# Two first loads of the second graph pass, converted to fp32r by GpSimd's transfers on their way from DRAM

## The chip, the cores and the metric

The kernel runs on one core of one Trainium2 chip. A core has TensorE (matmul), VectorE, ScalarE, GpSimd and SyncE, which work side by side and wait for each other on semaphores, and 16 DMA engines that serve the transfers issued by SyncE, ScalarE and GpSimd. The metric is the device time of one execution in microseconds (us), the median of the runs shown. In the profile PE is TensorE, PEld its weight loads, DVE is VectorE, ACT is ScalarE, POOL is GpSimd, SP is SyncE; SPq, ACTq and POOLq are the DMA issues of an engine.

## The reference

Two layers of a graph network over 6250 nodes of 128 features and 206,250 edges, each behind a layer norm and a relu, each added to its input.

```python
h = jnp.maximum(_layernorm(x, axis=-1), 0.0)
x = x + _L0_gnn_ref(h, src, dst, W, b)       # deg**-0.5 scaling, sum over edges, relu, @ W.T + b
h = jnp.maximum(_layernorm(x, axis=-1), 0.0)
x = x + _L1_gnn_ref(h, [src, dst], edge_type, ...)
# _L1_gnn_ref:
msg = h[src] @ W_msg.T + b_msg + edge_embed[clip(edge_type, 0, 8)]
messages = segment_sum(msg, dst, 6250)
return gru_cell(messages, h, W_ih, W_hh, b_ih, b_hh)
```

## The kernel before, in words

The sums over edges are done as matrix products. The nodes are padded to 6272, which is 49 blocks of 128. The kernel builds the 6272 x 6272 matrix of edge counts (`adj`) once, in bf16, from one-hot rows on TensorE, and uses it twice.

**First pass.** It goes through the destination columns in 25 tiles: one of 128 and 24 of 256 columns. For each tile the counts are built, copied to SBUF by ScalarE (L855), widened to fp32r in seven pieces of seven source blocks (`wide1`, L947, by VectorE and ScalarE in turn; the seventh piece, `wide_last`, by a GpSimd transfer, L943), and multiplied (L811) with the first table `tab1`, whose seven tiles each hold seven source blocks in two terms (an fp32 value split in two fp32r numbers): 14 matmuls for each piece. The counts are also stored to DRAM as `adj_d` (L954, by SyncE), cut into 13 tiles of destination columns for the second pass: one of 384, eleven of 512 and one of 256. L868, L872 and L876 end the first layer for a tile, L881 adds its result to `xs`, and L883 to L900 compute the norm's mean and scale.

**Second pass.** For each of the 13 tiles (`BACK`), `blocks(c, nd)` gives a function `block(q)` that brings piece q, seven source blocks by the tile's columns: a load from `adj_d` by SyncE into `piece` (L1007, one of four buffers), then a conversion to fp32r into `wide` (one of three buffers) by VectorE (L1018) or, after the first tile and for even q, by ScalarE (L1011). Row sums of the counts (`leave`, L999) are taken beside it for a final consistency test. `sums` multiplies the pieces with the second table `tab2` (L811): 7 pieces x 14 matmuls for a tile. A GRU cell follows for each tile: h from the table (L1051), its transpose (L1055, copied by L1057 to `hT`), products with `whh_sb` (L1061), with the type counts (L1071) and with the sums (L1066, L1073), two sigmoids (L1078, L1079), a tanh (L1085), elementwise steps (L1081 to L1090), a transpose back (L1094), the addition (L1096) and the store (L1101). `second_layer` is a generator whose stages are laid among the next tile's matmuls.

**Between the passes.** The second table is made from `xs` in seven steps: seven ScalarE activations (L1030) for each, then a VectorE cast (L1031) and a VectorE subtraction (L1032). After steps 1, 3 and 5 the kernel calls `first(0)`, `first(1)` and `first(2)`, the first tile's pieces 0, 1 and 2; the other four are called from `sums`. `whh_sb` is loaded from ScalarE's queue at L1036.

**What sets the order.** In the second pass and between the passes, the order of the instructions of each engine is made by a scheduler when the program is built; in the first pass it is mostly as written. Waits follow from the tiles' memory: a tile placed over an earlier one waits until that one's last reader is done. The `wide` pool lies on the right side of SBUF, where `tab1` was. GpSimd issues only the indirect loads of the prologue and the 25 `wide_last` transfers before the seam, and none after it.

Of the kernel before, what the change touches and what calls it, by code (L numbers as in the profile page):

```python
# [12 lines left out]
F32R = mybir.dt.float32r  # L13
# [8 lines left out]
P = 128  # L22
# [24 lines left out]
HP = 7  # L47
# [225 lines left out]
def by_matrix(  # L273
# [22 lines left out]
    nc = tc.nc  # L296
# [8 lines left out]
    adj_d = [dram.tile([P, NB, n], BF16, name=f"adj_d{c}") for c, (_, n) in enumerate(BACK)]  # L305
# [85 lines left out]
    with tc.tile_pool(name="pro", bufs=1) as pro, tc.manual_schedule(engines={mybir.EngineType.DVE}):  # L391
# [13 lines left out]
        for c in range(NCH):  # L405
            lo, hi = c * CB, min((c + 1) * CB, full)
            nc.sync.dma_start(
                out=xs[:, lo:hi, :], in_=x[lo * P : hi * P, :].rearrange("(b p) f -> p b f", p=P)
# [30 lines left out]
        for h in range(2):  # L439
            nc.gpsimd.indirect_dma_start(  # L440
                out=span[:, h, :],
                out_offset=None,
                in_=dst.rearrange("p t -> (p t)").unsqueeze(1),
# [68 lines left out]
        for k0 in range(0, NT // P + 1, 4):  # L512
# [26 lines left out]
            if n == P:  # L539
                nc.sync.dma_start(  # L540
                    out=flat[k0 * P : k1 * P, :].rearrange("(k p) e -> p k e", p=P),
                    in_=turned[:, k0:k1].rearrange("p k h f e -> p k (h f e)"),
# [281 lines left out]
    with tc.tile_pool(name="adj_even", bufs=1, reuse_waits="tile") as adj_even, tc.tile_pool(  # L824
        name="wide1", bufs=3, reuse_waits="tile"
    ) as wide1p, tc.tile_pool(
        name="ev_ps", bufs=1, space=PSUM, reuse_waits="tile"
# [158 lines left out]
    with early_p as tab2a, tc.tile_pool(name="gru_a", bufs=2, reuse_waits="tile") as gru_a, tc.tile_pool(  # L986
        name="tab2b", bufs=1, reuse_waits="tile"
    ) as tab2b, tc.tile_pool(name="f2_p", bufs=2, reuse_waits="tile") as f2p, tc.tile_pool(
        name="back", bufs=4, reuse_waits="tile"
    ) as backp, tc.tile_pool(name="gru", bufs=2, reuse_waits="tile") as gru, tc.tile_pool(name="wide", bufs=3, side="right", reuse_waits="tile") as wide, tc.tile_pool(  # L990
        name="gate_ps", bufs=1, space=PSUM
# [6 lines left out]
        def row_sums(q, c, piece):  # L998
            nc.vector.tensor_reduce(leave[:, q * HP : (q + 1) * HP, c], piece, AX.X, ALU.add)  # L999

        def blocks(c, nd):
            pieces = {}

            def block(q):
                if q not in pieces:
                    piece = backp.tile([P, HP, 512], BF16, name="piece")
                    nc.sync.dma_start(out=piece[:, :, :nd], in_=adj_d[c][:, q * HP : (q + 1) * HP, :])  # L1007
                    pieces[q] = wide.tile([P, HP, 512], F32R, name="wide")
                    if c > 0 and q in BY_ACT:
                        for i in range(HP):  # L1010
                            nc.scalar.activation(  # L1011
                                pieces[q][:, i, :nd],
                                piece[:, i, :nd],
                                AF.Copy,
                                accum_out=leave[:, q * HP + i, c : c + 1],
                            )
                    else:
                        nc.vector.tensor_copy(pieces[q][:, :, :nd], piece[:, :, :nd])  # L1018
                        if c > 0:
                            row_sums(q, c, piece[:, :, :nd])  # L1020
                return pieces[q]

            return block

        first = blocks(0, BACK[0][1])
        for c in range(NCH):
            f = f2p.tile([P, CB, H], F32, name="f2")
            for k in range(CB):
                b = c * CB + k
                nc.scalar.activation(f[:, k, :], xs[:, b, :], AF.Relu, bias=sh[:, b : b + 1], scale=rstd[:, b : b + 1])  # L1030
            nc.vector.tensor_copy(tab2[c][:, 0], f)  # L1031
            nc.vector.tensor_tensor(tab2[c][:, 1], f, tab2[c][:, 0].bitcast(F32), ALU.subtract)  # L1032

            if c in (1, 3, 5):
                first(c // 2)
        nc.scalar.dma_start(out=whh_sb, in_=whhT)  # L1036

        def second_layer(d0, nd, acc):
# [104 lines left out]
def gnn_kernel(tc, *args):  # L1143
    with tc.tile_pool(name="bad", bufs=1) as pool:
        bad_i = pool.tile([P, 1], I32, name="bad_i")
        by_matrix(tc, bad_i, *args)
        general(tc, bad_i, *args)
# [47 lines left out]
```

## Time and profile before

| what | value |
|---|---|
| median of 3 runs | 931.22 us (930.29 to 931.83) |
| profiled execution, its own time | 934.99 us |
| its span | 933.2 us |
| granted TensorE clock over the span | 0.96 |
| TensorE busy | 852.5 us (91%) |
| VectorE busy | 799.1 us (86%) |
| ScalarE busy | 712.3 us (76%) |
| GpSimd busy | 54.6 us (6%) |
| DMA q1 (SyncE) / q0 (GpSimd), share of 16 engines | 60.5% / 7.9% |

The busy shares are averages over stages with different limits: a prologue of about 110 us, the first pass to about 551 us, the second pass from there. What an edit between the passes is worth has to be read from the stretch around 550 us and from whether TensorE has idle time after it. In the slices of the page each digit is the busy share of one fortieth of the span in tenths; PEclk is the clock that TensorE was granted.

### The profile page before, as it was taken

The page shows a single profiled execution, that of the slowest core. Times are in us where ns is not written, and L with a number is a line of the kernel's source. Part 1 is how long each engine was busy: PE and PEld are TensorE (multiplying, and loading weights), DVE is VectorE, ACT ScalarE, POOL GpSimd, SP SyncE. Part 2 cuts the span into 40 slices and gives each one's busy share as a digit, 9 for nine tenths or more (in the row PEclk, how much of TensorE's full clock was granted, in tenths as well). Part 3 has the DMA queues.
Part 4 walks back from the last instruction along what each step waited for, and adds up shares of the span by engine and source line. Part 5 has one row for each costly group of instructions (what it writes and reads, how often), then busy time and mean ns, then how long its engine had stood idle before and what let it go on. Part 6 is the DMA issues. An engine that isn't in the chain of part 4 may idle for free.

```text
span 933.2 us, 24704 instructions
## 1 busy us (share of the span) xinstructions
PE 852.5 (91%) x10859; PEld 717.7 (77%) x10859; DVE 799.1 (86%) x835; ACT 712.3 (76%) x1205; POOL 54.6 (6%) x103
## 2 busy tenths in 40 slices
PE   3566499999998999999999979999999999999995
PEld 3354399998997999899999979776777777777775
DVE  5869999999999999999999768998888888877754
ACT  2277898999898899899999984776667676675752
POOL 4561000000000000000000000000000000000000
PEclk9579699999999999999999989999999999999998
DMA  9430177787787689678688798776777667766640
GB/s 283 126 105 32 40 185 238 221 264 232 221 263 233 186 250 276 191 235 273 203 244 274 216 313 289 257 267 211 279 281 243 234 239 264 266 216 225 212 128 23
DMA packets 205664, 203.72 MB, mean 218 GB/s; under 512 B 11178, under 2 KB 190881, under 8 KB 205393
## 3 DMA queue, kind: packets, MB, share of 16 engines
q1 hardware_dynamic: 198904, 173.34, 60.5%
q0 software_dynamic: 6032, 27.43, 7.9%
q8 instruction: 86, 1.41, 0.6%
q10 hardware_dynamic: 612, 1.30, 0.4%
q14 instruction: 30, 0.25, 0.1%
HBM read 95.68 MB, written 83.87 MB: 192 GB/s over the span
## 4 chain that ended last, share of the span: by engine, by line
PE 64%; ACT 14%; DVE 10%; issue 6%; DMA 4%; POOL 1%; another core or an unknown queue 0%; DVEq 0%; SPq 0%; ACTq 0%; POOLq 0%
PE acc L811 45%; ACT adj L855 8%; PE ev L843 7%; DMA piece<-adj_d 3%; ACT wide L947 3%; PE gate L1073 3%; PE gate L1061 3%; DVE wide L1018 2%; PE acc L876 2%; DVE leave L999 1%; PE turn L681 1%; DVE fields L672 1%; ACT f L1030 1%; PE sums L710 1%; DVE hot_l L353 1%
## 5 line engine op out<-in xcount | busy, mean ns | idle before, releaser
L811 PE MATMUL acc<-wide,tab 128*128 128x256 f32 (+2 forms) x3374 | 580.9, 327 | 4.3 <-issue 2.2
L811 PEld LDWEIGHTS acc<-wide,tab 128*128 128x128 f32 x3374 | 489.5, 189 | 65.6 <-issue 13.6
L855 ACT CAST adj<-ev 128x1960 bf16<-128x1960 f32 (+2 forms) x221 | 282.5, 1340 | 35.9 <-PE ev L843 19.9
L1011 ACT ACTIVATE wide<-piece 128x512 fp32r<-128x512 bf16 (+1 forms) x336 | 200.9, 601 | 63.5 <-issue 33.9
L353 DVE TENSOR_TENSOR hot_l<-lo_t,iota 128x3840 bf16<-128x3840 bf16 (+2 forms) x109 | 223.4, 2050 | 5.8 <-PE ev L843 5.7
L999 DVE TENSOR_REDUCE leave<-piece 128x7 f32<-128x3584 bf16 (+2 forms) x43 | 154.9, 3602 | 23.5 <-DMA piece<-adj_d 23.4
L947 ACT CAST wide<-adj 128x1792 fp32r<-128x1792 bf16 (+1 forms) x75 | 126.2, 1682 | 0.0
L843 PE MATMUL ev<-hot_c,hot_l 64*128 64x49 bf16 x6204 | 100.7, 182 | 7.1 <-DVE hot_c L353 3.6
L843 PEld LDWEIGHTS <-hot_l 64*128 64x128 bf16 x6204 | 88.5, 93 | 21.8 <-issue 4.4
L353 DVE TENSOR_TENSOR hot_c<-code_t,iota 128x1500 bf16<-128x1500 bf16 (+2 forms) x109 | 97.4, 893 | 0.0
L1018 DVE CAST wide<-piece 128x3584 fp32r<-128x3584 bf16 (+2 forms) x43 | 82.5, 1920 | 12.3 <-PE acc L811 12.3
L947 DVE CAST wide<-adj 128x1792 fp32r<-128x1792 bf16 (+1 forms) x75 | 80.5, 1087 | 14.4 <-ACT adj L855 13.6
L1011 ACT ACTIVATION_READ_ACCUMULATOR wide<-piece 128x1 f32 x336 | 63.2, 188 | 0.0
L1066 ACT COPY sum_sb<-acc 128x512 f32<-128x512 f32 (+2 forms) x13 | 7.3, 563 | 58.4 <-PE acc L811 58.4
L811 PE MATMUL acc<-wide_last,tab 128*128 128x256 f32 x350 | 48.2, 283 | 0.0
L811 PEld LDWEIGHTS acc<-wide_last,tab 128*128 128x128 f32 x350 | 43.6, 188 | 0.4
L943 POOL DMA_DIRECT2D wide_last<-adj x25 | 13.7, 550 | 447.4 <-PE acc L811 207.9
L1073 PE MATMUL gate<-sum_sb,wsum_sb 128*128 128x512 f32 (+2 forms) x78 | 35.0, 585 | 0.1
L1061 PE MATMUL gate<-hT,whh_sb 128*128 128x512 f32 (+2 forms) x78 | 33.7, 567 | 0.0
L681 PE MATMUL turn<-ident_b,fields 128*128 128x128 bf16 x225 | 20.6, 275 | 13.7 <-DVE fields L672 10.3
L681 PEld LDWEIGHTS <-fields 128*128 128x128 bf16 x225 | 19.0, 128 | 15.8 <-DVE fields L672 12.1
L650 POOL DMA_INDIRECT got<-flat,row_i x25 | 27.4, 1098 | 14.7 <-DVE m_dve L706 7.7
(167 smaller groups left out, 504.4 us busy)
## 6 DMA issues: line engine op xcount, KB each, us to landing
adj_d<-adj SPq DMA_DIRECT2D x24, 3136.0 KB
piece<-adj_d SPq DMA_DIRECT2D x77, 896.0 KB
wide_last<-adj POOLq DMA_DIRECT2D x24, 896.0 KB
piece<-adj_d SPq DMA_DIRECT2D x14, 672.0 KB
piece<-adj_d SPq DMA_DIRECT2D x7, 448.0 KB
out_dram<-res SPq DMA_DIRECT2D x11, 256.0 KB
xs<-in_x_dram SPq DMA_DIRECT2D x6, 448.0 KB
adj_d<-adj SPq DMA_DIRECT2D x1, 1568.0 KB
```

Of the source, the lines that this page charges most:

```text
L353: nc.vector.tensor_tensor(to.rearrange("p j (k t) -> p j k t", t=2), twice.unsqueeze(2).to_broadcast([P, n, m // 2, 2]), of[:, :m].rearran ...
L650: nc.gpsimd.indirect_dma_start(out=got[:, b].rearrange("p r f j -> p (r f j)"), out_offset=None, in_=edges_flat, in_offset=bass.IndirectOf ...
L681: nc.tensor.matmul(turns_[i][:, b, :], fields[:, b * ROWS + r, i].rearrange("p d j -> p (d j)"), ident_b, start=(r == 0), stop=(r == ROWS ...
L811: nc.tensor.matmul(acc[:, : 2 * P].rearrange("f (t n) -> f t n", t=2) if twice else acc[:, :nd], tab[:, s, i, :], a[:, i, :P].unsqueeze(1) ...
L843: nc.tensor.matmul(ps[:, d % banks, slot * NB : (slot + 1) * NB], hot_l[half, t + d // 2, :], hot_c[half, t + d // 2, :NB], start=True, st ...
L855: nc.scalar.copy(adjs[c][:, :, at : at + n].rearrange("p n (j d) -> p n j d", d=banks), ps[:, :banks, : n // banks * NB].rearrange("p d (j ...
L947: make(wides[c][q][:, :, :n], a)
L999: nc.vector.tensor_reduce(leave[:, q * HP : (q + 1) * HP, c], piece, AX.X, ALU.add)
L1011: nc.scalar.activation(pieces[q][:, i, :nd], piece[:, i, :nd], AF.Copy, accum_out=leave[:, q * HP + i, c : c + 1],)
L1018: nc.vector.tensor_copy(pieces[q][:, :, :nd], piece[:, :, :nd])
L1061: nc.tensor.matmul(ps[:, :nd], whh_sb[:, g * H : (g + 1) * H], hT[:, :nd], start=True, stop=(g == 2))
L1073: nc.tensor.matmul(ps[:, :nd], wsum_sb[:, g * H : (g + 1) * H], sum_sb[:, :nd], start=False, stop=True)
```

## The change

For the first tile's pieces 0 and 1, `block` no longer loads bf16 with SyncE and converts with VectorE. It asks GpSimd for a transfer from `adj_d` in DRAM straight into `wide`, which converts bf16 to fp32r on the way. Both calls are placed ahead of the loop that makes the second table. The calls to `first` inside the loop are gone, so piece 2, which had one, is now brought where `sums` asks for it, as pieces 3 to 6 are. Pieces 2 to 6 of the first tile and all later tiles keep the load and the conversion.

```diff
             def block(q):
-                if q not in pieces:
+                if c == 0 and q < 2 and q not in pieces:
+
+                    pieces[q] = wide.tile([P, HP, 512], F32R, name="wide")
+                    nc.gpsimd.dma_start(out=pieces[q][:, :, :nd], in_=adj_d[c][:, q * HP : (q + 1) * HP, :])
+                elif q not in pieces:
                     piece = backp.tile([P, HP, 512], BF16, name="piece")
                     nc.sync.dma_start(out=piece[:, :, :nd], in_=adj_d[c][:, q * HP : (q + 1) * HP, :])
                     pieces[q] = wide.tile([P, HP, 512], F32R, name="wide")
...
         first = blocks(0, BACK[0][1])
+        for q in range(2):
+            first(q)
         for c in range(NCH):
...
             nc.vector.tensor_copy(tab2[c][:, 0], f)
             nc.vector.tensor_tensor(tab2[c][:, 1], f, tab2[c][:, 0].bitcast(F32), ALU.subtract)
-
-            if c in (1, 3, 5):
-                first(c // 2)
         nc.scalar.dma_start(out=whh_sb, in_=whhT)
```

In the built program the scheduler also moves other instructions of the second pass. In the first tile TensorE's order becomes: 14 matmuls of piece 0, one type product (L1071), two of the three products with `whh_sb` (L1061), the matmuls of pieces 1 to 5, the third L1061 product, piece 6; before, the three L1061 products stood together ahead of piece 6 and the type product ahead of piece 3. VectorE's copy of `hT` (L1057) stands after the cast of piece 2; before, it stood after the casts of pieces 0 to 4. On SyncE the loads of pieces 2 and 3, then the three of the type counts, then those of pieces 4 to 6 keep their order behind the two that are gone; since the four `piece` buffers now begin with piece 2, those of pieces 4 and 5 need not wait for a buffer. In tiles 8 to 11 the transposes of the gate output (L1094) stand 18 matmuls behind the L1073 products; before, 28.

## The prediction

> **What bounds the kernel now.** I read the slices and the costliest groups of the page first, then TensorE's waits and its busy time in stretches of the second pass, then the timeline of 547 to 580 us engine by engine, and last the DMA queues us by us. The page and the stretches say who sets the pace:
>
> ```profile
> PE   3566499999998999999999979999999999999995
> PEclk9579699999999999999999989999999999999998
> L811 PE MATMUL acc<-wide,tab 128*128 128x256 f32 (+2 forms) x3374 | 580.9, 327 | 4.3 <-issue 2.2
> 700.00:730.00 30.00, 30.00 (x125) 21.98 (x124) 25.51 (x16) 20.48 (x63) 0.00 (x0) 1.00 0.74 250
> PE tr L1094 <- DVE og L1090: 4.5, 5, 2.8
> ```
>
> The second pass is a queue on TensorE: 30.00 of 30.00 us busy, VectorE 25.5, ScalarE 20.5, DMA 0.74. From 578 us to the end TensorE waits five times, 4.5 us in all, always for the gate output. So a shift of the second pass's start is carried to the end, and work taken from VectorE later buys nothing. The seam between the passes is the one hole:
>
> ```profile
> 547.74 1.82 PE L811 MATMUL acc<-wide_last,tab 128*128 128x256 f32 x14
> 550.58 0.71 PE L876 MATMUL acc<-w_sb,rl 128*128 128x128 f32 x4
> 554.51 0.88 PE L1055 MATMUL tr<-ident,h 128*128 128x128 f32 x3 [3.22 <-DVE sh L893]
> 556.25 10.38 PE L811 MATMUL acc<-wide,tab 128*128 128x384 f32 x42 [0.87 <-DVE rstd L894]
> 566.82 7.69 PE L811 MATMUL acc<-wide,tab 128*128 128x384 f32 x42
> ...
> 553.81 0.55 DVE L1051 TENSOR_TENSOR h<-tab 128x384 f32<-128x384 f32 x1
> 554.28 0.16 DVE L893 TENSOR_TENSOR sh<-sh 128x4 f32<-128x4 f32 x1
> 554.35 1.75 DVE L1018 CAST wide<-piece 128x2688 fp32r<-128x2688 bf16 x1
> 556.02 0.15 DVE L894 SCALAR_TENSOR_TENSOR rstd<-sh,rstd 128x4 f32<-128x4 f32 x1
> ```
>
> Columns: start, duration, engine, line, operation, count. TensorE waits until 554.5 for h, then until 556.25 for the first cast of a piece. Equal groups of 42 matmuls then take 10.38 and 7.69 us. The clock column (last but two) says why:
>
> ```profile
> 552.00:552.25 0.25, 0.00 (x0) 0.00 (x0) 0.25 (x1) 0.25 (x2) 0.00 (x0) 0.69 1.10 326
> 561.75:562.00 0.25, 0.25 (x2) 0.25 (x2) 0.25 (x2) 0.25 (x2) 0.00 (x0) 0.50 1.09 338
> 562.25:562.50 0.25, 0.25 (x3) 0.25 (x2) 0.25 (x1) 0.22 (x1) 0.00 (x0) 0.83 0.41 126
> ```
>
> The granted clock falls to 0.50 at 552.1 and is back at 562.3.
>
> **The change, part by part.**
>
> *Removed.* Two loads of SyncE and two VectorE casts of 1.75 us (3.5 us), the first of which TensorE waits for. Its start now needs the transposes (554.51 + 0.88 = 555.39) and the landed transfer. VectorE's order up to h is the same in both builds, so the 554.5 stays. The second cast is worth nothing by itself: the matmuls of piece 1 follow those of piece 0 without a gap in the trace. Direct gain: 556.25 - 555.39 = 0.86 us.
>
> *Clock.* A 384-column matmul takes 7.69/42 = 0.183 us at full clock. In the group of 10.38 us, 4.3 us lie after 562.3 (23.6 matmuls), so 18.4 take 6.05 us: 0.33 us each. [...] I take 0.4, with ends 0 and 1.5.
>
> *Added: two GpSimd transfers.* In the built program the three wide buffers lie over blocks 1-2, 5-6 and 3-4 of the first table, taken in that order. So transfer 0 waits for the last matmul on block 2 (541.60 plus nine of 6.30/51 us: 542.7; SyncE's second load, which waits for block 3, goes out at 544.65, one block of 1.73 us later: 542.9). Transfer 1 waits for the last matmul of the first pass, 549.5. "Begun ahead of the second table" therefore holds for neither in time. Both wait behind nothing else on GpSimd: its last wide_last, issued 537.60, is before them. Issue:
>
> ```profile
> 112.77 1.00 POOL L943 DMA_DIRECT2D wide_last<-adj  x1 [35.78 <-ACT adj L855]
> 537.60 0.53 POOL L943 DMA_DIRECT2D wide_last<-adj  x1 [16.00 <-PE acc L811]
> q0 software_dynamic: 50, 0.36, 90.4%
> q0 software_dynamic: 16, 0.01, 4.5%
> ```
>
> The first row is the near one, since that transfer also has 896 rows: 1.0 us. The queue lines (packets, MB, share) are of 544 to 545 and 546 to 547: issued at 537.60, this queue moves its bulk from 544 and is done at 546.2, because SyncE's last store (25 KB packets) is ahead in the engines. The transfer of 112.77 starts near 117. So a start lag of 4.2 us; transfer 0 begins at 547.2.
>
> Duration: 896 rows of 768 B in, 1536 B out, 56 per engine. Plain loads run at 326 GB/s, giving 2.1 us as the lower bound. wide_last alternates with the loads packet by packet at about 390 GB/s written; a pair of 1536 + 768 B at 390/16 per engine is 94 ns, so 5.3 us for 56 with a load beside it. I take 5.3, upper end 6.6 (pairs of 118 ns, the two packets one after the other). Transfer 0: 547.2 + 5.3 + 1 for the receipt (wide_last: data to 546.2, used at 547.7 without a wait; 1 us is my estimate) = 553.5, needed at 555.4: hidden, 1.9 us to spare. Transfer 1: 549.6 + 4.2 + 5.3 + 1 = 560.1.
>
> [...]
>
> *Moved by the scheduler.* TensorE now does block 0 (14 matmuls), one type product and two of the three L1061 products, then block 1. Those need hT and whh_sb. VectorE: h ends 554.36, sh, tab L1031 (0.6), the piece-2 cast (1.75; its load is first behind the store on SyncE's queue and shares with transfer 0, landing about 552.6), small ones, tab L1032, tab L1031, hT: 559.2. TensorE arrives at 555.4 + 11 x 0.33 + 3 x 0.183 + 0.3 = 559.9, or 560.6 cold. whh_sb leaves ScalarE's queue 1 us earlier than at 556.21, as the L897 it stands behind does; in before its packets ended in 559 to 560, so about 559. Both hidden by 0.7 to 1.4 us; without that cover, up to 1 us. Then 4 x 0.35 for the two products: block 1 starts at 561.2, transfer 1 is there with 1 us to spare.
>
> On SyncE, the loads of pieces 2 and 3 move up to the places of 0 and 1 (535.89, 544.65); the type loads wait for L876 as before (551.37); pieces 4 and 5 find free buffers and follow at 552.4, where they went out at 556.13 and 558.54. They share the engines with transfer 1, land by 560 and are cast at 564 and 566.3, when wide buffers come free. Cover: 4 us.
>
> Blocks 1 to 6 and the third L1061 product, unhindered, take 6 x 14 x 0.183 + 0.7 = 16.1 us: end of tile 0 at 577.3 with the early clock, 578.2 cold, against 578.9 now (L1066 copies the sum at 578.95).
>
> *Later tiles.* The scheduler's order differs to the end. In tiles 8 to 11 the gate output's transposes (L1094) now stand 18 matmuls behind the L1073 products instead of 28. By ScalarE's three casts, two sigmoids, two casts and the tanh, then three VectorE steps of 0.68, og is ready 14.0 us into the tile; TensorE arrives at 13.65: up to 0.35 us x 4 = 1.4 us of stall. Against it, tile 2 loses 0.9 + 0.3 us at its L1094 now and tile 8 0.41; the new order leaves tile 2's transposes 38 matmuls of room. Net 0, ends -1.6 and +1.4.
>
> **Sum.** -0.86 - 0.4 + 0 = -1.3 us. The profiled execution is 934.99 (span 933.2, 1.8 around it), 3.8 above the median of 931.22; it becomes 933.7, the median 929.9.
>
> **Rivals.**
> *A, slower: transfer 1 becomes the wait.* It starts only at 549.6. If it lags as wide_last did (6.4 us, to 544.0) and runs at the upper 6.6 us, it lands at 563.6. [...] 2.4 + 1.5 - 0.86 = +3.0: 934.3. It decides from a landing at 561.2; beyond 562.1 the gain is eaten. For it: 1.38 MB written where 0.69 was, with the queue 0.90 to 1.1 busy until 554. Against: the 25 KB packets are gone by 546.
> *B, nothing left:* the start moves 0.86 us but the L1094 stalls of tiles 8 to 11 (1.4) come true: 931.4. Speaks for it: every trailing order with few matmuls of room stalled at least once (0.90, 0.22, 0.41).
> [...]
> *D, transfers hidden and also useless*, if h were late anyway: excluded for the first 0.86 us, since the transposes ended at 555.39 and only the cast held the product.
>
> **Chances and range.** Main case 0.37 (929.9), A 0.23, B 0.2, C 0.2. 0.2% is 1.9 us, about what a measurement of this kernel tells from no change. Faster by more: C and a third of the main case; slower: A; the rest between. Main's own range 928.8 to 931.0; with the others 927.3 to 934.3.
>
> **What would show it.** Right: the first second-pass matmul at about 555.4 and clock 1.00 again at 558.9 or 562.3; L1061 products after 14 matmuls without a wait; no wait of TensorE for a transfer to wide; tile 0 done 1 to 2 us earlier. Wrong: a TensorE wait before the 15th matmul (A, or whh_sb or hT late), VectorE's piece-2 cast beginning after 555 (its load held up by transfer 0), or L1094 waits in tiles 8 to 11 (B).

## The result, and the profile after

The changed kernel is slower: 934.71 us (932.31 to 939.16, 20 runs) against 930.47 us (927.63 to 932.71, 20 runs) for the kernel before on the same chip, a ratio of 1.0048 (95% interval 1.0038 to 1.0059). The forecast was 929.9 us with a range of 927.3 to 934.3. A second set of runs of the changed kernel gave 1.0056 (1.0043 to 1.0068).

From L1004 on, line numbers of the changed kernel are 3 or 4 higher than before's: L1061 is L1064 now, L1066 is L1069, L1071 is L1074, L1094 is L1097, L1036 (the load of `whh_sb`) is L1039, L1018 (VectorE's cast) is L1022, and the GpSimd transfer is L1008. In two of the experiments, hold and htro, the lines behind L1066 are another 2 higher: the `sum_sb` copy is L1071 there, the type product L1076, the last step of the gate output `og` L1095 and its transposes L1099. The profiled executions are alike in length (span 932.6 us, before 933.2), because the one shown of before ran 4.5 us above its median: its first pass ended 3.3 us later than this one's. So the stretches below are measured from the last L876, the end of the first pass, which starts at 550.58 before and at 547.30 here.

Of the page:

```profile
PE   3566499999999999999999979999999999999995
PEclk9589599999999999999999989999999999999998
L811 PE MATMUL acc<-wide,tab 128*128 128x256 f32 (+2 forms) x3374 | 581.7, 327 | 3.4 <-issue 2.2
```

A stretch of the second pass (us, busy us of PE, PEld, DVE, ACT and POOL, then clock, DMA share and GB/s):

```profile
700.00:730.00 30.00, 30.00 (x125) 21.79 (x124) 25.72 (x16) 20.27 (x64) 0.00 (x0) 1.00 0.73 249
```

TensorE's waits from 530 us on (in total, times, longest; the other two lines, for `sh` and `rl`, stand in before's list with the same 3.2 and 0.8 us):

```profile
PE tr L1097 <- DVE og L1093: 4.8, 6, 2.8
PE gate L1064 <- DMA whh_sb<-in_L_W_hh_t_dram: 2.1, 1, 2.1
```

TensorE still sets the pace. The last line is new: TensorE waits 2.1 us, once, for `whh_sb`. The seam's timeline shows where (TensorE, then VectorE):

```profile
547.30 0.71 PE L876 MATMUL acc<-w_sb,rl 128*128 128x128 f32 x4
551.23 0.87 PE L1058 MATMUL tr<-ident,h 128*128 128x128 f32 x3 [3.21 <-DVE sh L893]
551.75 4.45 PE L811 MATMUL acc<-wide,tab 128*128 128x384 f32 x14
556.14 0.33 PE L1074 MATMUL gate<-types,emb_s 27*128 27x384 bf16 x1
558.55 2.42 PE L1064 MATMUL gate<-hT,whh_sb 128*128 128x384 f32 x4 [2.08 <-DMA whh_sb<-in_L_W_hh_t_dram]
560.20 13.85 PE L811 MATMUL acc<-wide,tab 128*128 128x384 f32 x70
...
550.53 0.55 DVE L1054 TENSOR_TENSOR h<-tab 128x384 f32<-128x384 f32 x1
551.61 0.15 DVE L894 SCALAR_TENSOR_TENSOR rstd<-sh,rstd 128x4 f32<-128x4 f32 x1
551.68 1.75 DVE L1022 CAST wide<-piece 128x2688 fp32r<-128x2688 bf16 x1
555.09 0.55 DVE L1060 COPY hT<-tr 128x384 f32<-128x384 f32 x1
```

The transposes start 3.93 us after L876, as before. The first product follows at 4.45 us where it took 5.67: the hold by VectorE's cast is gone. Then comes the hole, right behind the first piece. `hT` is ready at 555.64, before it.

The hole costs more than its length. TensorE's busy time and clock by the us (columns: us, PE busy, clock, DMA share, GB/s):

```profile
554.30:555.30 1.00, 1.00 (x5) 0.50 1.12 326
555.30:556.30 1.00, 1.00 (x6) 0.84 1.10 326
556.30:557.30 1.00, 0.17 (x1) 1.00 1.10 333
557.30:558.30 1.00, 0.00 (x0) 1.00 1.09 344
558.30:559.30 1.00, 0.75 (x2) 0.87 1.10 327
559.30:560.30 1.00, 1.00 (x4) 0.50 1.09 326
561.30:562.30 1.00, 1.00 (x4) 0.50 1.07 418
562.30:563.30 1.00, 1.00 (x7) 0.92 0.82 330
```

A mean of 0.84 between 0.50 and 1.00 puts the rise at about 555.6, which is 8.3 us after L876 (before, 562.3, it was 11.7). The hole begins 0.8 us later and sends the clock down to 0.50 a second time, from about 559.0 to 562.5.

Why the load is late stands in the issues and the DMA queues. First the changed kernel's two GpSimd issues and ScalarE's issue of `whh_sb`, from the timeline:

```profile
539.96 1.09 POOL L1008 DMA_DIRECT2D wide<-adj_d  x1 [5.08 <-PE acc L811]
546.61 0.94 POOL L1008 DMA_DIRECT2D wide<-adj_d  x1 [5.56 <-PE acc L811]
551.87 0.36 ACTq L1039 DMA_DIRECT2D whh_sb<-in_L_W_hh_t_dram  x1
```

Its queues (packets, MB, share) in 551.87 to 552.87, in 554 to 556 and in 556.87 to 557.87:

```profile
q0 software_dynamic: 246, 0.38, 169.3%
...
q1 hardware_dynamic: 844, 0.63, 107.7%
q0 software_dynamic: 28, 0.03, 5.8%
...
q10 hardware_dynamic: 131, 0.18, 54.6%
q1 hardware_dynamic: 215, 0.16, 53.5%
```

Then the kernel before, 557 to 560, its load having been issued at 556.21:

```profile
q1 hardware_dynamic: 736, 0.56, 65.9%
q10 hardware_dynamic: 139, 0.19, 17.2%
```

q10 is ScalarE's queue, with `whh_sb` in it. In the changed kernel only q0 moves in the first us after the issue: that is transfer 1. Then come the pieces on q1, and only 5 us after the issue does q10 move its bulk. TensorE's wait ends 6.55 us after the issue, when the last of the load's 16 completion signals comes. In the kernel before the DMA engines stood idle at its issue (one packet in the 0.7 us ahead of it); its packets ran 1.8 to 4.3 us after it, and the last signal came 4.9 us after it (4.5 in the second profile of before).

### The profile page after: what moved, and what is told of

It is laid out like the page before. It is cut to its first block, busy times and chain, and to the rows that moved or that the text cites. A ratio compares the mean times of both kernels' runs of the same rounds, so it can differ in the third digit from the quotient of the medians.

```text
span 932.6 us, 24708 instructions
## 1 busy us (share of the span) xinstructions
PE 851.7 (91%) x10859; PEld 715.7 (77%) x10859; DVE 797.2 (85%) x833; ACT 711.4 (76%) x1205; POOL 56.6 (6%) x105
## 4 chain that ended last, share of the span: by engine, by line
PE 61%; ACT 14%; DVE 11%; issue 6%; DMA 6%; POOL 1%; DVEq 0%; SPq 0%; POOLq 0%; ACTq 0%
PE acc L811 43%; ACT adj L855 8%; PE ev L843 7%; DMA piece<-adj_d 4%; PE gate L1064 3%; PE gate L1076 2%; ACT wide L947 2%; DVE wide L1022 2%; PE acc L876 2%; DVE hot_l L353 2%; POOL got L650 1%; DVE fields L672 1%; DVE leave L999 1%; ACT f L1036 1%; DMA dst_i<-in_dst_dram 1%
## 5 line engine op out<-in xcount | busy, mean ns | idle before, releaser
L1022 DVE CAST wide<-piece 128x3584 fp32r<-128x3584 bf16 (+2 forms) x41 | 79.1, 1930 | 21.8 <-PE acc L811 21.5
L1069 ACT COPY sum_sb<-acc 128x512 f32<-128x512 f32 (+2 forms) x13 | 7.3, 563 | 55.1 <-PE acc L811 55.1
L1064 PE MATMUL gate<-hT,whh_sb 128*128 128x512 f32 (+2 forms) x78 | 34.8, 581 | 2.1 <-DMA whh_sb<-in_L_W_hh_t_dram 2.1
L1076 PE MATMUL gate<-sum_sb,wsum_sb 128*128 128x512 f32 (+2 forms) x78 | 35.0, 585 | 0.1
L681 PE MATMUL turn<-ident_b,fields 128*128 128x128 bf16 x225 | 18.7, 259 | 14.3 <-DVE fields L672 14.3
```

The costliest lines, as they stand in the source:

```text
L681: nc.tensor.matmul(turns_[i][:, b, :], fields[:, b * ROWS + r, i].rearrange("p d j -> p (d j)"), ident_b, start=(r == 0), stop=(r == ROWS ...
L1064: nc.tensor.matmul(ps[:, :nd], whh_sb[:, g * H : (g + 1) * H], hT[:, :nd], start=True, stop=(g == 2))
L1076: nc.tensor.matmul(ps[:, :nd], wsum_sb[:, g * H : (g + 1) * H], sum_sb[:, :nd], start=False, stop=True)
```

## The experiments

For each profile the table has the time from the start of the last L876 to the `sum_sb` copy (L1066, L1069 or L1071) of the first tile, which ends that tile, and of the last tile. Ratios are to the kernel before on the same chip, estimated from all runs; and not quotients of medians. The kernel before was run again beside each set; its medians there were 930.47, 930.60, 930.85 and 930.15 us.

| kernel | to tile 0's end, us | to the last tile's end, us | median, us | ratio (95%) |
|---|---|---|---|---|
| before | 28.37 | 370.65 | 930.47 | |
| before, again | 28.35 | 368.91 | 931.67 | 1.0010 (0.9995 to 1.0025) |
| changed | 29.91 | 373.31 | 934.71 | 1.0048 (1.0038 to 1.0059) |
| changed, again | 30.05 | 373.79 | 936.46 | 1.0056 (1.0043 to 1.0068) |
| hold | 26.58 | 369.32 | 931.57 | 1.0002 (0.9989 to 1.0014) |
| wsum | 26.62 | 370.05 | 930.39 | 0.9996 (0.9983 to 1.0009) |
| early | 25.93 | 367.58 | 930.94 | 0.9999 (0.9989 to 1.0009) |
| one | 25.77 | 369.15 | 929.69 | 1.0000 (0.9987 to 1.0013) |
| two | 28.09 | 369.27 | 931.92 | 1.0017 (1.0006 to 1.0029) |
| etro | 26.18 | 367.28 | 929.30 | 0.9986 (0.9970 to 1.0002) |
| etro2 | 25.98 | 367.00 | 928.03 | 0.9975 (0.9961 to 0.9988) |
| htro | 26.72 | 366.76 | 927.44 | 0.9973 (0.9960 to 0.9986) |
| btro | 28.15 | 368.70 | 930.67 | 1.0001 (0.9986 to 1.0016) |
| otro | 25.29 | 366.24 | 928.44 | 0.9981 (0.9969 to 0.9992) |

Two halves of the edit were not timed. With the two calls ahead of the table but SyncE's loads and VectorE's casts kept, the built program has the same order of instructions on every engine as before; with the GpSimd transfers called at the old places it has the changed kernel's. So by the order of instructions the place of the calls does nothing, and the transfers are the whole change.

**Hold the products back (hold).** TensorE's order of the first tile is undone at one place, all else stays.

```diff
-                nc.tensor.matmul(ps[:, :nd], whh_sb[...], hT[:, :nd], start=True, stop=(g == 2))
+                hh = nc.tensor.matmul(ps[:, :nd], whh_sb[...], hT[:, :nd], start=True, stop=(g == 2))
+                if d0 == 0:
+                    tc.keep_in_program_order(hh)
```

> The changed kernel, but tile 0's three L1064 products on TensorE are held behind the products of piece 5, where the kernel before has them; the GpSimd transfers and every other engine's order stay. Theory 1 (the products came up behind the first piece and waited 2.08 us for whh_sb, and the hole chilled the clock a second time, about 1.5 us): no L1064 wait, the granted clock doesn't fall a second time at the first tile, and the time falls by about 3.6 us to about 931 (ratio to the kernel before 1.0003 to 1.0015). Theory 2 (the loss is in the later tiles' order and in what the GpSimd transfers do to other transfers): the ratio stays at 1.003 or more, and the seam to the last transposes stays 2 us or more above the kernel before's 375.4 us.

Measured 931.57 us, ratio 1.0002. The timeline of TensorE:

```profile
552.50 0.87 PE L1058 MATMUL tr<-ident,h 128*128 128x128 f32 x3 [3.22 <-DVE sh L893]
553.02 4.83 PE L811 MATMUL acc<-wide,tab 128*128 128x384 f32 x14
558.08 12.63 PE L811 MATMUL acc<-wide,tab 128*128 128x384 f32 x70
570.55 2.10 PE L1064 MATMUL gate<-hT,whh_sb 128*128 128x384 f32 x6
```

And its clock by the us (us, PE busy, clock, DMA share, GB/s):

```profile
557.60:558.60 1.00, 1.00 (x5) 0.85 1.12 344
558.60:559.60 1.00, 1.00 (x8) 1.00 1.07 344
563.60:564.60 1.00, 1.00 (x8) 1.00 1.01 351
```

No wait, no second cold stretch; the first tile ends 3.3 to 3.5 us sooner than in the changed kernel, and 1.8 us sooner than in the kernel before. Theory 1 holds for the larger part. But the kernel before is not beaten: the ratio is 1.0002, and the last tile's end, at 369.3 us, lies between before's two profiles (370.65 and 368.91), so the later tiles lose about what the first one gains. Theory 2 has a part too.

**Other weights, already there (wsum).**

```diff
-                    ps[:, :nd], whh_sb[:, g * H : (g + 1) * H], hT[:, :nd], ...
+                    ps[:, :nd], (whh_sb if d0 else wsum_sb)[:, g * H : (g + 1) * H], hT[:, :nd], ...
```

> The changed kernel, but tile 0's three L1064 products read wsum_sb, which is in SBUF since the prologue, in place of whh_sb (so tile 0's recurrent part is computed from other weights). They still come up right behind the first piece, but have nothing to wait for. Theory 1 (the wait and the second cold clock window): no wait, the clock stays up once risen, about 3.6 us less than the changed kernel, about 931 us. A rival (it is the place of the three products itself, in the middle of the pieces, and not their wait): the time stays near 934.7, ratio 1.004 to 1.006.

Measured 930.39 us, ratio 0.9996. All three products stand right behind the first piece here (in the changed kernel two of the three do). TensorE has no idle time before them: they begin 9.5 us after L876, and `hT` has been ready since 8.3. The first tile ends at 26.62 us, as in hold. Their place costs nothing; what they waited for does.

**The load earlier (early).**

```diff
+        nc.scalar.dma_start(out=whh_sb, in_=whhT)
         first = blocks(0, BACK[0][1])
...
-        nc.scalar.dma_start(out=whh_sb, in_=whhT)
```

> The changed kernel, but the load of whh_sb is traced ahead of the second table, so that it issues on ScalarE in the middle of the table's activations, some 2 us earlier than in the changed kernel (at about 3 us after the last L876 instead of 4.6). Theory 1: it lands at or before the first piece's end; the wait shrinks from 2.1 us to 0 to 0.5 and the second cold window is gone, time about 931 to 931.5. A rival (the load cannot land before the GpSimd transfer's packets have gone, because all 16 DMA engines are full of them till 5.5 to 6 us after the seam's start): it lands no earlier than about 556 on the changed kernel's clock, a wait of 0.5 to 2 us stays, and the time is 932 to 935.

Measured 930.94 us, ratio 0.9999. ScalarE's issue, from the timeline, and the first tile on TensorE:

```profile
549.59 0.36 ACTq L1029 DMA_DIRECT2D whh_sb<-in_L_W_hh_t_dram  x1
553.24 4.57 PE L811 MATMUL acc<-wide,tab 128*128 128x384 f32 x14
557.65 2.17 PE L1064 MATMUL gate<-hT,whh_sb 128*128 128x384 f32 x6
559.37 21.84 PE L811 MATMUL acc<-wide,tab 128*128 128x384 f32 x112
```

The issue came 0.8 us after the start of L876 (548.78), earlier than the 3 expected. By the queues q10 moved its bulk 5 to 7 us after the issue, once more only when transfer 1 was nearly through (110 of 144 packets in 6 to 7). So the rival was right that the load does not pass the transfer here: its last completion signal comes 8.7 us after L876, which is the rival's 556 on the changed kernel's clock. It was wrong in this profile that a wait remains, but nothing is to spare, since the products begin at 8.87 us. etro2 below, with the same order at the seam and an earlier clock, has an L1064 wait of 0.5 us in its profile. Moving the load also changed the scheduler's order: all three L1064 products stand behind the first piece, with no type product ahead of them, and `hT` is ready 1.4 us earlier. So early shows that an earlier load removes the wait, but it is not a change of the load alone.

**The changed kernel again (again).**

> The changed kernel once more, for a second profile and its ratio on the same chip as the other three. Ratio to the kernel before 1.0038 to 1.0059 as recorded. In the profile the L1064 wait is there again (1.8 to 2.4 us) if it is part of the program's timing and not of one execution; the lengths from the last L876 to the sum_sb copies of the tiles repeat to within 0.3 us except where the clock's rise falls in another place.

936.46 us. The wait is there again, 2.43 us, and the first tile's end repeats (30.05 against 29.91). It belongs to the program. Tiles 2 and 3 do not repeat to the 0.3 us expected (29.47 and 29.97 us in the first profile, 29.92 and 29.41 here).

**The kernel before again (bagain).**

> The kernel before once more, for a second profile. Its first one needed 28.37 us from the last L876 to tile 0's sum_sb copy, and with tile 0's wait gone the changed kernel needs 26.6 us. If the first profile fell into a long cold stretch of the clock (about 10 us at 0.50 there), this one shows a shorter one and 26.8 to 27.8 us to sum_sb, and the rest of the second pass repeats to 0.5 us; if 28.4 is what this order takes, it repeats to 0.2 us. Ratio to the kernel before 1.000.

I thought that the 28.37 us might be an unlucky cold stretch. They repeat, 28.35 here, and so do the 42 matmuls of 10.38 us:

```profile
550.82 0.87 PE L1055 MATMUL tr<-ident,h 128*128 128x128 f32 x3 [3.22 <-DVE sh L893]
552.56 10.37 PE L811 MATMUL acc<-wide,tab 128*128 128x384 f32 x42 [0.87 <-DVE rstd L894]
563.12 7.68 PE L811 MATMUL acc<-wide,tab 128*128 128x384 f32 x42
```

By themselves the two profiles could share their luck, since in both the clock fell 1.5 us after L876 and came back 11.7 us after it. The profile of btro below, which is the kernel before at the seam, settles it: there the clock fell at 4.4 and came back at 11.3 us, and the first tile took 28.15 us.

What did not repeat are small losses in later tiles. Tile 2 took 30.52 us in the profile shown with the prediction and 29.84 here, tile 8 30.02 and 29.40. The last tile's end differs by 1.7 us between the two profiles of one program.

**One transfer each (one, two).**

```diff
-                if c == 0 and q < 2 and q not in pieces:
+                if c == 0 and q < 1 and q not in pieces:      # one
+                if c == 0 and q == 1 and q not in pieces:     # two
```

> Only the first of the two loads goes by a GpSimd transfer, piece 1 is loaded and cast as before. TensorE's order then has tile 0's three L1064 products behind piece 5, and no L1074 product before them, so nothing of tile 0 waits for whh_sb. Theory 1 (the loss is the products' wait for whh_sb, whatever makes the transfers): the direct gain is kept, no L1064 wait, 930 to 931.5 us. The rival (each GpSimd transfer of 1.38 MB costs by itself, through the DMA engines it shares): half the loss stays, 932.5 to 933.

> Only the second of the two loads goes by a GpSimd transfer; piece 0 is loaded and cast as before. TensorE's order has the L1074 product behind piece 0 and the three L1064 products behind piece 5. Theory 1: no L1064 wait, and no direct gain, since the first product again waits for VectorE's cast of piece 0 (5.4 to 5.7 us after the last L876 instead of 4.45): 931 to 931.5 us. The rival (each transfer costs by itself): 932.5 to 933. If the transfer comes too late, TensorE waits for wide at piece 1, as was forecast for the slower side.

With the first alone the scheduler leaves the three products behind piece 5; no L1064 wait, the best first tile of the two (25.77 us), ratio 1.0000. A price of each transfer by itself, half the loss, would be 1.0024; the interval ends at 1.0013. With the second alone the first product comes 5.67 us after L876, as before, so there is no direct gain, and no L1064 wait; 1.0017 (1.0006 to 1.0029) is above what I expected and does not exclude the rival by its time. Its profile shows no new wait, and the last tile's end 0.4 us behind the second one of before; its tiles 8 to 11 take 29.6 us each where before's take 29.4, which is more than that. The load's landing was not the same in these two: issued while q1 alone was busy, q10's packets began 2.2 and 2.3 us after the issue, against 1.8 with idle engines (before) and 4.8 behind transfer 1 (changed).

**The later tiles (etro, htro, btro, otro, etro2).** In tiles 8 to 11 the changed kernel takes 29.60 us each, before 29.40 (a tile's length is the time from the last tile's `sum_sb` copy to its own). The edit holds the first transpose of `og` behind piece 3's products, in the tiles where it stood 3 or 4 products into that piece:

```diff
-                if k < 4 and before is not None:
+                if k in (0, 1, 3, 4) and before is not None:
                     run(before, 1)
...
-                nc.tensor.transpose(o_ps[...], o[...], ident)
+                turned = nc.tensor.transpose(o_ps[...], o[...], ident)
+                if k == 0 and 0 < d0 < BACK[-1][0]:
+                    tc.keep_in_program_order(turned)
```

etro and etro2 are this on early, htro on hold, otro on one, btro on the kernel before.

> The kernel with the early load of whh_sb (measured 930.9), and besides the first transpose of og held on TensorE behind the products of piece 3 in the tiles where it stood 3 or 4 products into piece 3 (tiles 4, 7 and 8 to 11), with the same calls one stage later in the program. Theory on the later tiles (tiles 8 to 11 take 29.60 us each against 29.40 where the transposes stand behind piece 3, and tile 7 30.2 against 29.5, because the transposes wait for og): 29.4 us a tile, 1.2 to 1.6 us less than with the early load alone: 929.3 to 929.8, the best of these kernels. A rival (the 0.2 us are the output's store or something else at the tile's seam): no change, 930.9.

> The kernel that holds tile 0's L1064 products behind piece 5 (measured 931.6), with the first transpose of og also held behind the products of piece 3 in tiles 4, 7 and 8 to 11, as in the kernel with the early load. This is the change with both of its side effects on TensorE's order taken out. Theory (what is left of the loss after the wait is the later tiles' order, 2.2 us by the tiles' lengths: 0.6 in tile 4, 0.8 in tile 7, 0.2 in each of 8 to 11): the last sum_sb copy at 367.1 to 367.4 us after the last L876 (369.3 with the hold alone, 368.9 in the second profile of the kernel before), and 929.3 to 929.8 us, ratio 0.998 to 0.9993. If the later tiles' loss is not their order: 931 to 931.6, ratio 1.000 to 1.001.

> The kernel before with the same hold of og's transposes behind piece 3 (it bites in two tiles only, where they stood 3 products into piece 3). A control: if the gain of this hold is its own and has nothing to do with the change, the kernel before gains too. Its tiles take 29.4 to 29.5 us already, so I expect no more than 0.2 us: ratio 0.999 to 1.001. If it falls to 0.9985 or below, the best version owes nothing to the GpSimd transfers.

> Only the first of the two loads by a GpSimd transfer, and the hold of og's transposes behind piece 3. The sum by tiles: 369.15 us to the last sum_sb copy with the first load alone, less 0.5 in tile 4 and 0.8 in tiles 8 to 11: about 367.8, and 928.5 to 929.5 us (ratio 0.998 to 0.999). If the second transfer is what brings the gain, it stays at 930 or more.

> The kernel with the early load of whh_sb and the hold of og's transposes once more, for its interval (0.9986, 0.9970 to 1.0002 the first time) beside the other three on one chip. Expected: 0.9975 to 0.9995; the tiles' lengths repeat to 0.4 us in all (367.3 us to the last sum_sb copy).

htro is the change with both side effects on TensorE's order taken out: 927.44 us, ratio 0.9973 (0.9960 to 0.9986), better than expected. Tiles 8 to 11 take 29.41 us, tile 7 29.40 where hold took 30.23, tile 4 29.40 for 30.07. What TensorE lost there was only partly listed as a wait for og. The transposes (L1099 in both), idle time of TensorE's matmuls and weight loads before them by releaser (us, times), of hold:

```profile
  issue: 8.1, 10
  DVE og L1095: 4.4, 5
```

and of htro:

```profile
  issue: 4.1, 4
  DVE og L1095: 3.0, 2
```

Idle time under "issue", in which the profile names no releaser, fell with the waits when the transposes stood further back. One tile of hold shows that it was a late og as well:

```profile
824.81 0.69 DVE L1095 TENSOR_TENSOR og<-og,ng 128x512 f32<-128x512 f32 x1
825.62 0.42 PEld L1099 LDWEIGHTS tr<-ident,og 128*128 128x128 f32 x4 [0.41 <-issue]
```

The weight load of the transposes begins 0.12 us after VectorE's last step on og, and the 0.41 us of idle time before it stand under "issue".

In tiles 8 to 11 the order explains the loss: every profile with 18 matmuls of room takes 29.6 us there, every one with 28 takes 29.4 (but for tile 8 in before's first profile, 30.02). In tiles 4 and 7 it does so only in part. two has the same 17 matmuls of room there as hold, and its tiles 4 and 7 take 29.46 and 29.44 us, because og is done 0.6 and 0.8 us earlier in the tile; in early it is tile 4 that loses nothing. So little room lets a late og through, and the hold removes the loss; why og is late in those two tiles was not tried.

btro, the control, gains nothing (1.0001): the kernel before has its transposes 3 products into piece 3 in two tiles only, and of its two profiles one has a wait of 0.2 us there and the other none. etro's interval reached 1.0002; etro2, the same kernel, gave 0.9975 (0.9961 to 0.9988). otro gave 0.9981. So htro, etro2 and otro beat both kernels, the kernel before by 1.7 to 2.7 us; between them the intervals overlap. otro has only the first transfer, so that the second adds anything is not shown.

One thing more in htro, on TensorE behind the first piece:

```profile
555.66 0.33 PE L1076 MATMUL gate<-types,emb_s 27*128 27x384 bf16 x1
556.71 12.63 PE L811 MATMUL acc<-wide,tab 128*128 128x384 f32 x70 [0.72 <-DMA wide<-adj_d]
```

With nothing else ahead of it, piece 1 does wait for transfer 1, by 0.7 us in this profile, in which the last signal of the transfer came 9.6 us after L876. In hold it came at 8.3 us, and TensorE, whose clock stayed at 0.50 until 9.3 us, asked for the piece only at 9.5. Over the eight profiles with both transfers it came 8.3 to 9.6 us after L876.

## Why the prediction was wrong

**The direct gain: right, a little small.** The forecast was 0.86 us for the cast that no longer holds the first product. In the profile the first product came 1.22 us earlier, since it did not wait for the end of the transposes as the profile draws it (552.10), which the forecast had as its start; it began at 551.75. The clock's part was put at 0.4 us, with ends 0 and 1.5: no run shows these, and they were the author's estimate. In their place the runs showed a clock that came back 11.7 us after L876 before, 9.3 in hold and 8.3 and 7.9 in the changed kernel's two profiles, the first three with the first product at 5.67, 4.45 and 4.45 us. In hold the products thus spend 1.2 us less at the clock of 0.50 than before; a 384-column matmul takes 0.183 us at full clock and 0.33 at 0.50 (before), so that full clock saves 1 - 0.183/0.33 = 0.445 of that time, 0.5 us (an estimate). That makes 1.8 us in all, where the forecast had 1.3; hold, without the wait, ends the first tile 1.8 us sooner than before.

**The two transfers: right that they are in time, with errors that cancel.** Transfer 0 was hidden: its last signal came 3.2 us after L876 (forecast 2.9) and the first product at 4.45. The margin was thin in other profiles, 4.4 us in htro. Transfer 1 was to land at 560.1, which is 9.5 us after the L876 of that profile. In the changed kernel it landed at 8.3 us. The start lag taken from `wide_last` served well; that the transfer would alternate with loads did not happen, it ran nearly alone at 0.37 to 0.38 MB per us (551 to 552.87 in the changed kernel) and so took less than the 5.3 us given. That htro has the forecast's 9.5 almost to the point (9.6) is luck, made by one late signal. Rival A's mechanism, transfer 1 as the wait, did not occur in the changed kernel: the transfer was there before TensorE was through with the type product at 9.2 us.

**`whh_sb`: the step that failed.** The prediction put: "whh_sb leaves ScalarE's queue 1 us earlier than at 556.21 ...; in before its packets ended in 559 to 560, so about 559. Both hidden by 0.7 to 1.4 us; without that cover, up to 1 us." The issue came at 4.57 us after L876 (5.63 before), so that part was right. Two things were wrong in the landing. It was read off the packets, most of which had run by 560 in before; the last completion signal came at 561.1, 4.9 us after the issue. Moved up by the 1 us, that is 560.1, already on the point of the need. And it was moved along with the issue, as if the load took the same time after any issue. It took 6.55 us instead of 4.9, since transfer 1 (1.38 MB) and the loads of two pieces, issued 2.7 and 2.3 us earlier, stood ahead of it. And the prediction knew the lag: it gave transfer 1 4.2 us of start behind a busy queue, and then did not apply it to the load that follows on another queue. With it the sum would have been, as an estimate: issue at 555.2, 4.2 us of lag (the one taken from `wide_last`), 2 us for the packets (before moved 0.19 of the 0.20 MB in 558.2 to 560.2), so 561.4 against the need at 559.9, a stall of 1.5 us. The need itself was right: TensorE was through with the type product 9.2 us after L876, which is 559.8 on the forecast's clock, and `hT` was ready 8.3 us after it (558.9, forecast 559.2). That the clock would be back after 11 of the 14 matmuls was the author's estimate; in the changed kernel it came back 3.9 us after the first product, which is about the time of 11 or 12 at 0.33 us. The landing was 11.1 us after L876, 561.7 where 559 was forecast. A late `whh_sb` stands in the prediction's list of what would show it wrong, without a price or a chance of its own.

**The price of a stall: too low.** "Up to 1 us" had no second cold stretch in it, though rival A's sum did: 2.4 us of stall (563.6 less 561.2) and 1.5 for the clock, a term that was an estimate and that no run shows as it stands. Measured: 2.1 and 2.4 us of wait, and 3.3 and 3.5 us of loss at the first tile's end against hold. The remaining 1.0 to 1.2 us is the second fall of the clock, less what hold lost because its clock first came back later (9.3 us after L876 against 8.3 and 7.9). With that counted by the 0.445, the second fall cost about 1.7 us in both profiles (an estimate), near rival A's 1.5. By its length, 3.4 us at 0.50 in the changed kernel (559.04 to 562.45), it would be 3.4 x 0.445 = 1.5 us.

**Later tiles: rival B's mechanism, at about 2 us.** The forecast was net 0, with 1.4 us of stall in tiles 8 to 11 against 1.2 us of relief in tile 2. The stall is real but smaller there, 4 x 0.2 us; tiles 4 and 7 add 0.6 and 0.8 us, in hold as in the changed kernel. The relief was none: tile 2's losses were of one execution, and the second profile of before lacks most of them. Of these 2.2 us the 0.8 in tiles 8 to 11 are shown to be the order; in tiles 4 and 7 og is also later than in two, for a reason that stays open.

The sum by these terms: -1.8 us at the start, +3.4 for the wait with its clock, +2.2 for tiles 4, 7 and 8 to 11, in all +3.8 us. The medians are 4.24 us apart. So the wait for `whh_sb` alone turns the forecast gain into a loss, and the later tiles make up the rest. The changed kernel's tile 1 is also 0.5 us longer than hold's (29.07 and 29.21 against 28.62), with an og wait of 0.2 to 0.4 us in it; why og is later there was not tried.

## What to carry to other kernels

When a large transfer is moved ahead, list every load that is issued after it, on any queue, and give each the backlog that then stands before it, up to its completion signal and not only to its packets; here the 192 KB of `whh_sb` became the wait although its issue had moved 1.1 us closer to L876 (4.57 us behind it instead of 5.63), because it took 6.55 us instead of 4.9. Read the new instruction order for consumers that the scheduler has pulled forward, and compare their need with that landing. Here the gain at one place, 1.8 us, was eaten by the order that came with it: pinning two kinds of instruction turned 4 us of loss into 2 to 3 us of gain.

## What the runs showed of the hardware

- In the changed kernel the small load of `whh_sb` on ScalarE's queue got no share of the engines while a large GpSimd transfer issued before it was under way. Its 192 KB had its packets 1.8 to 4.3 us after the issue with idle engines (before), 2.2 to 4.7 us behind plain loads (one, two), and 4.8 to 7.4 us behind a transfer of 1.38 MB (changed, early); in the first two us after the issue in the changed kernel q0 moved 0.38 and 0.36 MB and q10 nothing. Another pair of queues did share: SyncE's load of a piece, issued 1.4 us after transfer 0, moved beside it (changed: q0 1.02 MB and q1 0.40 MB in 545.3 to 549.3 us). What decides between the two was not tried.
- The GpSimd transfer that widens bf16 to fp32r wrote 0.37 to 0.38 MB per us while alone (q0 in 551 to 552 and 551.87 to 552.87 us of the changed kernel, 0.37 in two); at that rate 1.38 MB take 3.6 to 3.7 us (an estimate).
- In the changed kernel, after a hole of 2.1 us in TensorE's work, begun 0.8 us after the clock had come back, the clock was down at 0.50 again for about 3.4 us (559.04 to 562.45). After holes of 0.5 us (etro2) and 0.7 us (htro), begun 0.4 and 1.3 us after it had come back, it did not fall.
- The same program's later tiles differ by up to 0.7 us between executions (tile 2 of the kernel before: 30.52 and 29.84 us). Its first tile repeats to 0.02 us where the clock falls at the same place, the changed kernel's to 0.14 and etro's to 0.2 where it does not.
